# Small-head attention of a decoder: keys spread by unit of scores, values in halves behind the first scores, softmax sums inverted by batches

## The chip, the cores and the metric

The kernel runs on one core of a Trainium2 chip. The metric is the device time of one execution in microseconds. The kernel is one program for a whole decoder of four layers; the change touches three of its twelve stages.

## The reference, cut to what matters

Eight sequences of 56 tokens, width 256, pass through four layers of attention, cross-attention and feed-forward, each followed by a residual addition and a layer norm. The change touches the two attentions of layer 1 and the attention of layer 2. All of them are softmax attentions with many small heads:

```python
def _L1_attn_ref(...):                  # 32 heads of 8
    result, ch_bias, n = _chunk_decompose(hidden_states.reshape(bsz * tgt, H))
    def proj(w_orig, w_dq_t, b):
        y = result @ w_dq_t + ch_bias @ w_orig.astype(jnp.float32).T
        return y.reshape(-1, H)[:n] + b
    Q = (proj(q_weight, WQ, q_bias) * scaling).reshape(bsz, tgt, HEADS, HEAD_DIM)
    K = proj(k_weight, WK, k_bias).reshape(bsz, tgt, HEADS, HEAD_DIM)
    V = proj(v_weight, WV, v_bias).reshape(bsz, tgt, HEADS, HEAD_DIM)
    attn = jnp.einsum('bqhd,bkhd->bhqk', Q, K)
    probs = jax.nn.softmax(attn, axis=-1)
    ctx = jnp.einsum('bhqk,bkhd->bqhd', probs, V).reshape(bsz * tgt, H)
    r2, cb2, n2 = _chunk_decompose(ctx)
    out = (r2 @ WO + cb2 @ o_weight.astype(jnp.float32).T).reshape(-1, H)[:n2] + o_bias

def _L1_xattn_ref(q, latent_kv, Wq, Wkv_expand, Wout):     # 16 heads of 16
    qp = q @ Wq.T
    kv = latent_kv @ Wkv_expand.T       # keys and values come from a context of width 64
    ...                                 # causal softmax attention
    return out @ Wout.T

def _L2_attn_ref(x, q_w, kv_w, c_w):    # 16 heads of 16, 4 key/value heads
    ...                                 # rotary embedding of q and k, causal softmax attention
    return out @ c_w.T
```

`_chunk_decompose` cuts the 448 tokens into 14 chunks of 32, subtracts from each chunk and channel the middle of its range (`ch_bias`), and quantises the rest to int4 and back. A projection is then the product of the quantised residual with the quantised weight, plus the product of the 14 middles with the original weight, plus a bias.

## The kernel before, in words

**Layout.** Tokens lie in four tiles of 112 (two sequences each). `xT` holds the activations with channels on partitions, 128 x 2 x 448. PSUM has eight banks; in these three stages two pairs of banks (`bank2`) and two single banks (`bank`) turn around, and two banks hold the running output `ps_o`.

**Projections of the first stage** (`l1_attn`). `decompose` makes the residual `res` and the middles. `middles` multiplies the middles with the original weights and adds the bias: one product at a time, 14 rows, into `gb`, which is zeroed to 128 rows so that it can serve as a third term of every projection with `sel` (which chunk a token belongs to). The projection gives k, then q, each in two halves of 128 channels.

**Masked keys.** With heads of 8 or 16 channels a TensorE product over one head alone would use few rows. So `head_keys` builds `KX`: every key repeated once per head of a group and multiplied by a mask (`hm8`, `hm16`) that keeps the channels of one head. VectorE makes the first half of the sequences and POOL the second. `head_values` does the same for values: products for all eight sequences into `ps_v`, copied into a zeroed `VX` by ScalarE and VectorE.

**The loop** (`small_heads`) runs over units. A unit is a tile (two sequences) and, with heads of 8, one half of the channels: 8 units in the first stage, 4 in the two others. `scores(n)` forms the scores of a unit in PSUM, then VectorE takes maxima (`mx`) and subtracts them (`E`), ScalarE takes the exponent in place, VectorE sums (`sums`). `turned(n)` transposes the unit on TensorE and copies it to `eT`; `outputs(n)` multiplies with `VX` into `ps_o`. In program order, TensorE does scores n+1, the transposes of n, the outputs of n−1. `keep_in_program_order` fixes this order of TensorE; the other engines' orders, and where other TensorE work goes between, come from a list scheduler that estimates times. `ordered` fixes an instruction behind the one that precedes it on its engine.

**Behind the loop** all sums are inverted at once (128x128), transposed (`ps_rec`), spread into a block form `recT` by four scalings, and multiplied with a `spread` matrix into `ps_den`, the reciprocals by channel and token; VectorE multiplies them with the outputs into `oT`.

**Around it.** `finish` does the output projection (`ps_y`, tile by tile), residual addition and statistics, then `norm` (the L417 to L422 steps on few elements, the normalisation of X at L459), then `turn_x`, the transposition into `xT`. The second stage, `l1_xattn`, begins with the key projection from the context (`ps_k`), its masks and values, and the query projection from `xT`. `l2_attn` projects q and k with and without swapped pairs, multiplies with the tables (`d`, VectorE) and adds (POOL). Weights of a stage are loaded on the SP queue while the stage before runs.

Of the kernel before, what the change touches and what calls it, by code (L numbers as in the profile page):

```python
# [9 lines left out]
F32 = mybir.dt.float32  # L10
# [134 lines left out]
def _pack(i):  # L145
# [41 lines left out]
    w["l1a_s"] = _beside(_spread(8), (np.arange(T)[None, :] // 32 == np.arange(T // 32)[:, None]).astype(np.float32))  # L187
# [77 lines left out]
class Decoder:  # L265
# [1060 lines left out]
    def head_values(self, pool, terms, dk, groups=16):  # L1326


        nc = self.nc
        n, per = groups * dk // 2, 4  # L1330
        VX = pool.tile([128, NB, 128 // dk, 32], F32, bufs=1, name="VX")
        nc.gpsimd.memset(VX, 0.0)
        for g in range(NB // per):
            ps = self.bank("ps_v")
            for i in range(per):
                both = [terms(g * per + i, odd) for odd in range(2)]
                for k in range(len(both[0])):
                    for odd in range(2):
                        lhsT, rhs = both[odd][k]
                        nc.tensor.matmul(  # L1340
                            ps[odd * 64 : odd * 64 + S, i * n : (i + 1) * n], lhsT, rhs,
                            start=k == 0, stop=k == len(both[0]) - 1,
                        )
            for odd in range(2):
                rows = slice(odd * 64, odd * 64 + S)
                copy = nc.vector.tensor_copy if odd else nc.scalar.copy
                to, of = VX[rows, g * per : (g + 1) * per], ps[rows, : per * n]
                if dk == 8:
                    to = to.rearrange("p b (x y) n -> p (b x) y n", y=2)
                    of = of.rearrange("p (z y n) -> p z y n", y=2, n=8)  # L1350
                    for y in range(2):
                        at = 16 * y + 8 * odd
                        copy(to[:, :, y, at : at + 8], of[:, :, y, :])
                else:
                    same = 16 // groups
                    to = to.rearrange("p b (x y) n -> p (b x) y n", y=same)[:, :, :, 16 * odd : 16 * odd + 16]
                    of = of.rearrange("p (z n) -> p z n", n=16).unsqueeze(2).to_broadcast([S, per * groups // 2, same, 16])
                    copy(to, of)
        return VX

    def head_keys(self, pool, k, dk):

        nc, n = self.nc, 64 // dk
        KX = pool.tile([128, 2, NB, n, S], F32, bufs=1, name="KX")
        hm = self.const(f"hm{dk}").unsqueeze(1).unsqueeze(3).to_broadcast([128, NB // 2, n, S])
        for half in range(2):
            bs = slice(half * NB // 2, (half + 1) * NB // 2)
            for c in range(2):
                of = k[:, c, :].rearrange("p (b s) -> p b s", s=S)[:, bs].unsqueeze(2).to_broadcast([128, NB // 2, n, S])
                (nc.gpsimd if half else nc.vector).tensor_tensor(KX[:, c, bs], of, hm, ALU.mult)  # L1370
        return KX
# [7 lines left out]
    def small_heads(self, pool, q, KX, VX, dk, causal, scale, spread, oT):  # L1379
# [11 lines left out]
        num = pool.tile([128, 2, T], F32, bufs=1, name="num")  # L1391
# [59 lines left out]

        scores(0)
        for n in range(len(units)):
            if n + 1 < len(units):
                scores(n + 1)
            turned(n)
            if n:
                outputs(n - 1)
        outputs(len(units) - 1)
        rec = sums.rearrange("p t i -> p (t i)")  # L1460
        nc.vector.reciprocal(rec, rec)
        ps = self.bank("ps_rec")
        nc.tensor.transpose(ps[:, :128], rec, ident)
        recT = pool.tile([128, NT, 2, S], F32, bufs=1, name="recT")
        of = ps[:, :128].rearrange("p (u q) -> p u q", u=2)[:, :, :S]
        for t in range(NT):
            nc.vector.tensor_scalar_mul(recT[:, t], of, self.const("blocks")[:, t : t + 1])
        nc.scalar.copy(num, acc[:, :, :T])
        for c in range(2):
            ps = self.bank("ps_den")  # L1470
            self.mm(ps[:, :T], [(spread[:, c * 128 : (c + 1) * 128], recT.rearrange("p t u q -> p (t u q)"))])
            nc.vector.tensor_tensor(oT[:, c, :], ps[:, :T], num[:, c, :], ALU.mult)
# [54 lines left out]
    def l1_attn(self):  # L1527
# [6 lines left out]
        spread, sel = self.fields("l1a_s", D, T)  # L1534
        with tc.tile_pool(name="l1a", bufs=2) as pool:
# [20 lines left out]
            def middles(mid, first, n):  # L1556

                out = pool.tile([128, n, D], F32, bufs=1, name="gb")
                nc.gpsimd.memset(out, 0.0)
                ps = self.bank2("ps_gb")  # L1560
                for j in range(n):
                    self.mm(
                        ps[:G, j // 2, j % 2 * D : (j % 2 + 1) * D],
                        [(mid[:, c * G : (c + 1) * G], wT(first + j, c)) for c in range(2)]
                        + [(self.ones[:1, :G], bias[:, (first + j) * D : (first + j + 1) * D])],
                        fixed=True,
                    )
                for j in range(0, n, 2):
                    m = min(2, n - j)
                    nc.scalar.copy(out[:G, j : j + m, :].rearrange("p j n -> p (j n)"), ps[:G, j // 2, : m * D])  # L1570
                return out

            mid = self.decompose(pool, self.xT, res)
            gb = middles(mid, 0, 3)
            q, k = self.head_queries(pool), pool.tile([128, 2, T], F32, bufs=1, name="k")
            for m in (1, 0):
                ps = self.bank2("ps_q1")
                for o in range(2):
                    at = slice(o * 128, (o + 1) * 128)
                    self.mm(ps[:, o, :T], [(dT[:, m, c, at], res[:, c, :]) for c in range(2)] + [(gb[:, m, at], sel)])  # L1580
                    if m:
                        nc.scalar.copy(k[:, o, :], ps[:, o, :T])
                    else:
                        nc.scalar.copy(q[:, o, :, :S], ps[:, o, :T].rearrange("p (b s) -> p b s", s=S))
            KX = self.head_keys(pool, k, 8)

            def value_terms(b, odd):
                at = slice(b * S, (b + 1) * S)
                own = lambda a: a.rearrange("p (x y n) -> p x y n", y=2, n=8)[:, :, odd, :]
                return [(res[:, c, at], own(dT[:, 2, c, :])) for c in range(2)] + [(sel[:, at], own(gb[:, 2, :]))]  # L1590

            VX = self.head_values(pool, value_terms, 8, 32)
            oT = pool.tile([128, 2, T], F32, bufs=1, name="oT1")
            self.small_heads(pool, q, KX, VX, 8, False, 8.0**-0.5, spread, oT)
            res2 = pool.tile([128, 2, T], F32, bufs=1, tag="res", name="res2")
            mid = self.decompose(pool, oT, res2)
            gb2 = middles(mid, 3, 1)
            self.finish(
                early=False,
                terms_of=lambda t: [(res2[:, c, self.tok(t)], dT[:, 3, c, :]) for c in range(2)] + [(sel[:, self.tok(t)], gb2[:, 0, :])]  # L1600
            )


    def l1_xattn(self):
        nc, tc, xT = self.nc, self.tc, self.xT
        wq, wo = self.fields("l1x_1", 512, 512)
        wk, wv, cT = self.fields("l1x_2", D, D, T)
        wq, wo = (a.rearrange("p (c n) -> p c n", c=2) for a in (wq, wo))
        (spread,) = self.fields("l1x_t", D)
        with tc.tile_pool(name="l1x", bufs=2) as pool:  # L1610
            q = self.head_queries(pool)
            k = pool.tile([128, 2, T], F32, bufs=1, name="k")
            qps, kps = self.bank2("ps_q"), self.bank2("ps_k")
            for o in range(2):
                self.mm(kps[:, o, :T], [(wk[:DC, o * 128 : (o + 1) * 128], cT[:DC, :])])
            nc.scalar.copy(k, kps[:, :, :T])
            KX = self.head_keys(pool, k, 16)

            def value_terms(b, odd):
                own = wv[:DC, :].rearrange("p (x y n) -> p x y n", y=2, n=16)[:, :, odd, :]  # L1620
                return [(cT[:DC, b * S : (b + 1) * S], own)]

            VX = self.head_values(pool, value_terms, 16)
            for o in range(2):
                at = slice(o * 128, (o + 1) * 128)
                self.mm(qps[:, o, :T], [(wq[:, c, at], xT[:, c, :]) for c in range(2)])
                nc.scalar.copy(q[:, o, :, :S], qps[:, o, :T].rearrange("p (b s) -> p b s", s=S))
            oT = pool.tile([128, 2, T], F32, bufs=1, name="oT")
            self.small_heads(pool, q, KX, VX, 16, True, 0.25, spread, oT)
            self.finish(lambda t: [(oT[:, c, self.tok(t)], wo[:, c, :]) for c in range(2)], early=False)  # L1630


    def l2_attn(self):
# [6 lines left out]
        with tc.tile_pool(name="l2a", bufs=2) as pool:  # L1640
# [12 lines left out]
            KX = self.head_keys(pool, k, 16)  # L1653
            terms = lambda b, odd: [(xT[:, c, b * S : (b + 1) * S], wv[:, c, :]) for c in range(2)]
            VX = self.head_values(pool, terms, 16, 8)
            oT = pool.tile([128, 2, T], F32, bufs=1, name="oT2")
            self.small_heads(pool, q, KX, VX, 16, True, 0.25, spread, oT)
            self.finish(lambda t: [(oT[:, c, self.tok(t)], wo[:, c, :]) for c in range(2)], early=False, turn=False)
# [240 lines left out]
```

## Time and profile before

| | |
|---|---|
| time, three runs | 1656.13, 1664.53, 1664.38 us (median 1664.38) |
| profiled execution | 1665.35 us, span 1663.1 us |
| mean granted TensorE clock | 0.926 |
| PE busy | 90% |
| VectorE, ScalarE, POOL busy | 66%, 38%, 19% |
| first touched stage, loop | 535 to 566 us |
| second touched stage, loop | 607 to 625 us |
| third touched stage, loop | 754 to 772 us |

The shares are means over the whole span. The three loops together last some 68 us, and in them no engine is full for long: they pass each unit from one to the next. The granted clock of TensorE is 1.00 or 0.50 in a single stretch of the trace, and 0.926 is its mean.

### The profile page before, as it was taken

To read this page: it belongs to the slowest core of one execution; us is meant where nothing else is said; L and a number is where in the kernel's file an instruction comes from. 1 tells how busy PE (TensorE), PEld (TensorE's weight loads), DVE (VectorE), ACT (ScalarE), POOL (GpSimd) and SP (SyncE) were. 2 spreads that over 40 slices of the span, in tenths; PEclk is the share of its full clock that TensorE was granted. 3 is DMA by queue.
4 is the path that set the end of the run, shared out by engine and by line. 5 is a ranking of instruction groups with operands and counts; after the bars stand their busy time and mean duration, and the time that the engine had idled before them with its cause. 6 is when DMAs were issued, how large, how long until landed. Compare 5 with 4: busy or idle time off the path is not lost.

```text
span 1663.1 us, 37875 instructions
## 1 busy us (share of the span) xinstructions
PE 1499.5 (90%) x16428; PEld 894.4 (54%) x16428; DVE 1095.2 (66%) x1793; ACT 625.2 (38%) x915; POOL 323.9 (19%) x302
## 2 busy tenths in 40 slices
PE   7989989999788678998989999899987978999898
PEld 4666435556644344565435555655555834555656
DVE  0575579999475855326569999635474239999633
ACT  2431245655312422103245556332343144566320
POOL 4711511212123010011521122101131000221200
PEclk9999979999897878999988999999997987999989
DMA  9523422323020001222332322121220361323100
GB/s 359 188 79 108 123 56 84 96 83 88 18 87 28 26 27 35 78 70 74 114 86 62 110 78 81 41 64 55 83 64 27 119 172 38 104 72 88 41 1 11
DMA packets 52088, 133.76 MB, mean 80 GB/s; under 512 B 20673, under 2 KB 21137, under 8 KB 51922
## 3 DMA queue, kind: packets, MB, share of 16 engines
q1 hardware_dynamic: 19906, 65.36, 12.0%
q10 hardware_dynamic: 28368, 50.25, 10.8%
q0 software_dynamic: 3648, 15.73, 2.9%
q8 instruction: 129, 2.11, 0.5%
q14 instruction: 37, 0.30, 0.1%
HBM read 119.06 MB, written 6.75 MB: 76 GB/s over the span
## 4 chain that ended last, share of the span: by engine, by line
PE 49%; DVE 9%; issue 8%; ACT 2%; DMA 1%; POOL 1%; ACTq 1%; DVEq 0%; POOLq 0%
PE ps_x L376 17%; PE ps_glu L368 8%; PE ps_y L368 7%; PE ps_qk L1675 2%; DVE sc L376 2%; PE ps_v L1675 2%; PE ps_qh L368 2%; PE ps_big L368 1%; PE ps_y L1675 1%; PE ps_q L368 1%; PE ps_qk L376 1%; PE ps_m L376 1%; PE ps_s L1397 1%; DVE E L1418 1%; DVE mx L1415 1%
## 5 line engine op out<-in xcount | busy, mean ns | idle before, releaser
L376 PE MATMUL ps_x<-kvT,qa 64*128 64x375 f32 x1344 | 310.4, 567 | 29.1 <-DVE sc L376 23.1
L376 ACT ACTIVATE sc<-sc,tops 128x1500 f32<-128x1500 f32 x168 | 259.2, 1544 | 151.7 <-DVE sc L376 118.3
L376 DVE STREAM_TRANSPOSE eT<-sc 128x1536 f32<-128x1536 f32 x168 | 297.1, 1768 | 11.7 <-PE ps_x L376 9.5
L376 PE MATMUL ps_x<-eT,kv 32*64 32x224 f32 x9024 | 257.7, 357 | 3.7 <-issue 3.2
L376 PEld LDWEIGHTS ps_x<-eT,kv 32*64 32x64 f32 x9024 | 197.6, 133 | 70.1 <-issue 59.8
L376 PEld LDWEIGHTS ps_x<-kvT,qa 64*128 64x128 f32 x1344 | 114.3, 201 | 187.2 <-DVE sc L376 160.4
L376 DVE TENSOR_SCALAR_CACHE_REDUCE sc<-ps_x 128x750 f32<-128x750 f32 x168 | 157.3, 936 | 38.4 <-PE ps_x L376 38.2
L376 DVE TENSOR_SCALAR_CACHE_REDUCE sc<-ps_x,tops 128x750 f32<-128x750 f32 x168 | 161.1, 959 | 1.3 <-PE ps_x L376 1.1
L376 POOL TENSOR_TENSOR eT<-eyes,sums 128x224 f32<-128x224 f32 x24 | 13.3, 555 | 453.6 <-DVE sums L376 453.6
L827 POOL TENSOR_TENSOR rope<-rope,turn 96x448 f32<-96x448 f32 x64 | 71.0, 1130 | 65.0 <-DVE turn L825 65.0
L824 DVE TENSOR_TENSOR rope<-ps_big,consts 96x896 f32<-96x896 f32 x32 | 34.8, 1086 | 58.4 <-PE ps_big L368 58.4
L1190 ACT ACTIVATE act<-ps_glu 128x448 f32<-128x448 f32 (+1 forms) x52 | 28.3, 544 | 111.7 <-PE ps_glu L368 108.4
L1194 DVE TENSOR_TENSOR act<-ps_glu,act 128x448 f32<-128x448 f32 x43 | 26.8, 624 | 65.2 <-ACT act L1190 65.1
L418 ACT ACTIVATE rstd<-rstd 112x3 f32<-112x3 f32 (+2 forms) x21 | 4.3, 204 | 166.2 <-DVE rstd L417 166.1
L624 DVE RECIPROCAL rec<-rec 128x896 f32<-128x896 f32 x8 | 46.0, 5753 | 27.0 <-ACT rec L623 27.0
L376 PE MATMUL ps_x<-wm,qa 128*112 128x128 f32 (+1 forms) x336 | 53.5, 318 | 9.7 <-DVE qa L376 9.7
L450 DVE TENSOR_TENSOR X<-X,ps_y 112x256 f32<-112x256 f32 x32 | 13.5, 421 | 70.6 <-PE ps_y L368 70.6
L376 PEld LDWEIGHTS ps_x<-wm,qa 128*112 128x112 f32 x336 | 45.2, 191 | 21.7 <-issue 11.2
L1758 POOL TENSOR_TENSOR qk<-qk,sw 128x896 f32<-128x896 f32 x16 | 33.3, 2083 | 101.3 <-DVE sw L1757 78.8
L376 POOL TENSOR_TENSOR qa<-num,rec 64x448 f32<-64x448 f32 x42 | 47.9, 1140 | 2.9
L754 ACT COPY qa<-ps_qk 64x448 f32<-64x448 f32 x48 | 25.3, 527 | 60.0 <-PE ps_qk L376 46.1
L376 POOL DMA_DIRECT2D kvT<-kvT x24 | 13.7, 573 | 122.7 <-DVE X L450 49.2
(410 smaller groups left out, 2424.2 us busy)
## 6 DMA issues: line engine op xcount, KB each, us to landing
kv<-kv ACTq DMA_DIRECT2D x288, 128.0 KB, 2.7
kvT<-kvT POOLq DMA_DIRECT2D x24, 384.0 KB, 3.5
qa<-qa ACTq DMA_DIRECT2D x24, 224.0 KB, 3.6
raw<-in_ctx ACTq DMA_DIRECT2D x6, 512.0 KB, 4.3
kv<-raw POOLq DMA_DIRECT2D x6, 512.0 KB, 4.2
kvT<-by POOLq DMA_DIRECT2D x6, 512.0 KB, 4.3
l0a_q<-in_l0a_q SPq DMA_DIRECT2D x4, 512.0 KB, 10.6
l0a_c<-in_l0a_c SPq DMA_DIRECT2D x4, 512.0 KB, 8.8
```

The lines of the kernel that those rows point to most:

```text
L368: ins = self.nc.tensor.matmul(out, lhsT, rhs, start=n == 0, stop=n == len(terms) - 1)
L376: call(*args, **kw)
L624: nc.vector.reciprocal(rec, rec)
L754: nc.scalar.copy(flat[rows, :, odd, h // 2 * S : (h // 2 + 1) * S], ps[rows, :T].rearrange("p (b s) -> p b s", b=NB))
L824: nc.vector.tensor_tensor(rope.rearrange("p a (b s) -> p a b s", b=NB), view, cos, ALU.mult)
L827: nc.gpsimd.tensor_tensor(rope[:, half, :], rope[:, half, :], turn[:, 1 - half, :], ALU.add)
L1190: nc.scalar.activation(act, ps[:m, 0, :T], AF.Silu)
L1194: nc.vector.tensor_tensor(act, ps[:m, 1, :T], act, ALU.mult)
L1397: tc.keep_in_program_order(nc.tensor.matmul(*args, **kw))
L1415: nc.vector.tensor_reduce(mx, view, AX.X, ALU.max)
L1675: tc.keep_in_program_order(nc.tensor.matmul(*args, **kw))
L1758: nc.gpsimd.tensor_tensor(qk, qk, sw, ALU.add)
```

## The change

It does the following in the three stages:

- **Middles**: the products for k, q and v lie in three groups of 32 columns of TensorE (rows 0, 32, 64 of the result), in three banks, their terms interleaved. `gb` is no longer zeroed; each projection's third term has 14 rows. `sel` is repeated every 32 rows for this.
- **Order in the first stage**: half of k, half of q, half of k, the first scores, half of q, the second scores, then the values of the first four sequences behind `scores(1)` and of the last four behind `scores(2)`.
- **Keys by unit**: VectorE makes `KX` of units 0 and 1 (both channel halves of the first two sequences) straight from PSUM; POOL makes units 2, 4 and 6; VectorE makes units 3, 5 and 7, each ordered into the loop. In the two stages with heads of 16, `KX` is made in eight parts: all on VectorE in the second stage, half on VectorE and half on POOL in the third.
- **Values**: all copies into `VX` on ScalarE.
- **Sums**: inverted tile by tile in the loop, transposed in four pieces into 32 rows, copied once, and multiplied with 32 rows of `spread`.
- **Context's keys and values** (`l1x_context`): made at the end of the first stage's attention, ahead of its second `decompose`; the pool of the second stage is opened before that of the first.

```diff
 # head_keys
-        for half in range(2):
-            bs = slice(half * NB // 2, (half + 1) * NB // 2)
-            for c in range(2):
-                of = k[:, c, :].rearrange("p (b s) -> p b s", s=S)[:, bs].unsqueeze(2).to_broadcast([128, NB // 2, n, S])
-                (nc.gpsimd if half else nc.vector).tensor_tensor(KX[:, c, bs], of, hm, ALU.mult)
-        return KX
+        def made(unit, of_, engine):
+            t, cs = (unit // 2, (unit % 2,)) if dk == 8 else (unit, range(2))
+            for c in cs:
+                of = of_(c).rearrange("p (b s) -> p b s", s=S)[:, 2 * t : 2 * t + 2]
+                engine.tensor_tensor(KX[:, c, 2 * t : 2 * t + 2], of.unsqueeze(2).to_broadcast([128, 2, n, S]), hm, ALU.mult)
+        return KX, made
 # head_values: made(g) is called for half g
-                copy = nc.vector.tensor_copy if odd else nc.scalar.copy
+                ...  nc.scalar.copy(to, of)
 # small_heads
+        keys(0)
         scores(0)
         for n in range(len(units)):
             if n + 1 < len(units):
+                if not n:
+                    keys(1)
                 scores(n + 1)
+            if n < 2:
+                VX = values(n)
             turned(n)
             if n:
                 outputs(n - 1)
+            if n + 2 < len(units):
+                keys(n + 2)
+            if n % per == per - 1:
+                nc.vector.reciprocal(sums[:, n // per], sums[:, n // per])
         outputs(len(units) - 1)
-        rec = sums.rearrange("p t i -> p (t i)")
-        nc.vector.reciprocal(rec, rec)
+        nc.scalar.copy(num, acc[:, :, :T])
         ps = self.bank("ps_rec")
-        nc.tensor.transpose(ps[:, :128], rec, ident)
...
+            tc.keep_in_program_order(nc.tensor.transpose(ps[:32, t * 128 : (t + 1) * 128], sums[:, t], ident))
+        recT = pool.tile([32, NT * 2, S], F32, bufs=1, name="recT")
+        nc.vector.tensor_copy(recT, ps[:32].rearrange("p (u q) -> p u q", q=64)[:, :, :S])
 # l1_attn
+            def middles(mid, ms):
+                out = pool.tile([128, D], F32, bufs=1, name="gb")
+                ps = self.bank2("ps_gb")
+                banks = [ps[:, 0], ps[:, 1], self.bank("ps_gb1") if len(ms) > 2 else None]
+                for k in range(3):
+                    for j, m in enumerate(ms):
+                        ...
+                        self.ordered(nc.tensor.matmul, banks[j][32 * j : 32 * j + G, :D], lhsT, rhs, start=k == 0, stop=k == 2)
+                for j in range(len(ms)):
+                    nc.scalar.copy(out[32 * j : 32 * j + G], banks[j][32 * j : 32 * j + G, :D])
+                return lambda j: (out[32 * j : 32 * j + G], sel[32 * j : 32 * j + G])
...
+            def keyed(o):
+                ps = projected(0, 1, o)
+                made(o, lambda c: ps[:, :T], nc.vector)
+                nc.scalar.copy(k[:, o, :], ps[:, :T])
+            def keys(n):
+                if n == 0:
+                    keyed(0)
+                    projected(1, 0, 0)
+                    keyed(1)
+                    for m in (2, 4, 6):
+                        made(m, lambda c: k[:, c, :], nc.gpsimd)
+                elif n == 1:
+                    projected(1, 0, 1)
+                elif n % 2:
+                    self.ordered(made, n, lambda c: k[:, c, :], nc.vector)
...
             self.small_heads(pool, q, KX, keys, values, 8, False, 8.0**-0.5, spread, oT)
+            self.l1x_context()
             res2 = pool.tile([128, 2, T], F32, bufs=1, tag="res", name="res2")
 # l1_xattn
+            for n in range(NT):
+                made(n, lambda c: k[:, c, :], nc.vector)
 # l2_attn
+            for n in range(NT):
+                made(n, lambda c: k[:, c, :], nc.gpsimd if n > 1 else nc.vector)
```

## The prediction

> **What bounds the kernel now.** I read the shares first, then the chain of waits through the changed stages, then VectorE's timeline and TensorE's clock by window. The page's first part:
>
> ```profile
> PE 1499.5 (90%) x16428; PEld 894.4 (54%) x16428; DVE 1095.2 (66%) x1793; ACT 625.2 (38%) x915; POOL 323.9 (19%) x302
> ```
>
> PE is busy for 90% of the span, but that is an average: the cross-attentions and the feed-forwards fill it. The three stages that the change touches lie at about 501–597, 597–639 and 736–779 us, some 180 us of 1663. The chain of waits there (start, duration, what):
>
> ```profile
> 508.94 8.32 PE ps_gb L368 x18
> 517.26 9.69 PE ps_q L368 x18
> ...
> 530.20 4.94 PE ps_v L1340 x86
> 535.14 1.66 PE ps_s L1397 x16
> ...
> 545.05 0.96 PE ps_s L1397 x8
> 546.03 1.09 DVE mx L1415
> 547.12 0.99 DVE sums L1420
> 548.11 1.01 DVE E L1418
> 549.14 0.96 ACT E L1419
> 550.14 1.09 PE ps_eT L1430 x8
> 551.24 0.57 PE ps_o L1397 x31
> 551.80 0.95 PE ps_s L1397 x8
> ...
> 592.96 0.70 DVE VX L1358
> 593.88 0.70 DVE VX L1358
> ...
> 597.82 3.35 PE ps_k L368 x4
> ```
>
> Up to 536 us PE alone sets the time: bias middles, key and query projections, values, scores. From there the softmax loop is a ring through all three engines: scores, maxima, the previous unit's sums, subtraction, exponent, transposes, outputs, scores. One turn is 551.80 − 545.05 = 6.75 us and serves two units: 3.37 each, of which VectorE has 3.09 (1.09 + 0.99 + 1.01). VectorE is nearly full in this loop and PE is not. The last three lines show two VX copies that VectorE makes inside the norm, and a key projection at the entry of the second stage: both leave this path.
>
> VectorE's timeline at the key masks:
>
> ```profile
> 522.64 2.03 DVE L1370 TENSOR_TENSOR KX<-k,consts 128x1792 f32<-128x1792 f32 x1 [7.31 <-ACT k L1582]
> 526.05 3.55 DVE L1370 TENSOR_TENSOR KX<-k,consts 128x1792 f32<-128x1792 f32 x1 [1.38 <-ACT k L1582]
> ```
>
> The same operation took 2.03 and 3.55 us; POOL made its own half of KX from 522.69 to 532.66. TensorE's clock by window (length, then busy time of PE, PEld, DVE, ACT, POOL, then the granted clock):
>
> ```profile
> 515.89:519.31 3.42, 3.42 (x6) 1.30 (x6) 0.00 (x0) 0.84 (x2) 0.00 (x0) 0.50 0.13 53
> 519.31:522.72 3.41, 3.41 (x6) 1.41 (x5) 0.08 (x1) 0.53 (x1) 0.03 (x1) 0.50 0.00 0
> 522.72:526.13 3.41, 3.41 (x11) 1.75 (x10) 2.03 (x2) 0.53 (x1) 3.41 (x1) 1.00 0.00 0
> ...
> 560.27:563.68 3.41, 1.68 (x41) 1.37 (x41) 2.40 (x4) 1.92 (x3) 0.00 (x0) 1.00 0.00 0
> 563.68:567.09 3.41, 2.62 (x73) 2.09 (x73) 2.75 (x6) 1.88 (x3) 0.00 (x0) 1.00 0.02 5
> ...
> 590.99:594.40 3.41, 1.48 (x28) 1.23 (x24) 2.94 (x8) 1.16 (x3) 1.62 (x5) 1.00 0.50 161
> 594.40:597.81 3.41, 1.76 (x8) 1.38 (x8) 1.55 (x5) 0.91 (x1) 0.00 (x0) 0.50 0.00 0
> ```
>
> The clock changes at multiples of 3.41 us. Two full windows at 0.50 stand before the rise; a window with PE 1.68 busy (49%) kept full clock for the next, one with 1.48 (43%) lost it.
>
> **The change part by part**, against the profiled execution (1665.35 us: span 1663.1 and 2.25 around it; the median shown is 0.97 lower).
>
> *Middles and start.* The POOL memset of gb (0.74) and that of VX (3.51) leave the norm ahead, where one X operation lasted 2.26 instead of 0.42; part of this remains since the VX memset is only moved. I take −0.7. The three middles in column groups no longer end behind the residual: it is ready at 515.33, ps_gb ended at 517.26, so the projections start up to 1.9 us sooner.
>
> *Order up front, tiled attention.* New PE order: k half 0, q half 0, k half 1, scores 0, q half 1, scores 1, values half 0, transposes 0, scores 2, values half 1. VectorE makes KX 0 and 1 straight from PSUM (128x896, nearest row mx from PSUM, 1.09), while ACT's key copies (0.53) wait for it; POOL makes 2, 4, 6 (2.5 each, half of its 5.03), ahead of need. I laid the operations out by hand with the durations shown. With the clock rising at 522.7, as it does now, scores 3 start at 542.1; they started at 545.05: −2.9.
>
> *Rule against row.* Two full windows precede the rise at 522.72. The Trainium skill, "TensorE: Matmul & The Clock Gate", "What's actually happening", says that one busy window of about 3.4 us is enough, free-running. The first of the two held 1.4 us of 14-column middles, so it may not have counted; with middles gone from it the rule gives a rise at 519.3 and scores 3 at 540.4 (−4.6). But a third of each projection's terms now has 14 rows instead of 128 zero-padded ones. I stay with the row; the rule's 1.7 goes into the range.
>
> *The loop.* VectorE's queue in the built program reads: sums 2, KX 3, mx 3, E 3, mx 4, sums 3, E 4, reciprocal, sums 4, KX 5, mx 5 and so on. KX 3, 5 and 7 (1.09 each, half of 2.03 with its start) stand behind the sums of the unit before and ahead of their own scores. So scores 5 wait for KX 5, KX 5 for sums 4, these for exponent 4. One turn becomes a single file: KX 1.12, scores 0.98, mx 1.12, E and mx 2.1, the interposed sums 1.0, E 1.1, exponent 1.0, sums 1.0, with their gaps 9.7 us for two units against 6.75. Queued behind the waiting KX are its own mx and all later ones; PE waits for scores, and its transposes follow. Two such turns (KX 3 to 5, 5 to 7): +5.9. VectorE has only 7.9 us of work per turn, so 1.8 of the 9.7 is waiting. At the end: of four reciprocals of 128x32 (estimate 0.35, from 0.33 for 128x28) only the last is on the path, in place of one of 0.95, and one copy of 32x448 (0.63) replaces four scalings (1.07); with the last turn's overlap −1.4. From scores 3 to oT: 29.4 against 24.9, +4.5.
>
> *Rule against row again.* PE then works 5.2 us of a turn of 9.7 (twice 0.96, 1.09 and 0.57), 54% on average, and by the layout rests for 3.9 in one piece ahead of scores 5 and of scores 7. The same page, "HAM oscillation — how this bites in real kernels", warns of idle gaps above about 3.4 us: by it both gaps cost the clock, a cold window each of transposes, outputs and scores, +3 to +4. By the rows only the share of a window counts, with its limit between 43% and 49%; a gap that falls across two windows may pass, and part of a cold window is waiting anyway. I go by the rows and take +2 (ends 0 and +4). Stage so far: −0.7 − 2.9 + 4.5 + 2.0 = **+2.9**.
>
> *Context's keys and values.* k projection, values and four VX copies (0.58 each, ACT) move between oT and the second decompose, where PE waits 4.9 us for VectorE: nothing, while the top transpose (due 574.18) stands behind under 4 us of them; without that cover up to +1. ACT is free there. But in the norm chain VectorE now has eight KX of 128x448 (estimate 0.55–0.63, from 1.09 for twice as much) between X of the last tile, its statistics and the reciprocal: +4.4. Gone from there: two VX copies (−1.4), and of the 0.92 of L417, waiting beside POOL's memset, 0.75. Net **+2.1**; ends 0 (if statistics wait for ps_y anyway) and +3.
>
> *Entry of the second stage.* The 3.35 us of ps_k before ps_q are gone: −3.35. But these were the busy time that let the second query half run at 1.77 instead of 3.35, and KX is no longer the wait: I give back 2.4, for a later rise through scores 0 and transposes 0. **−0.95**; ends −3.4 and +1. Its loop: four reciprocals +0.5, end −0.45, **+0.2**.
>
> *Rope attention.* Rows of now: values 752.51 to 754.44, scores 0, E 1 at 759.16, scores 2 at 760.1. Values now come behind scores 1; the four VX copies (0.58) stand on ACT between exponent 0, exponent 1 and the transposes' copies, VectorE's half is lost, and transposes 1 wait for a bank until those copies are through: scores 2 at 762.7, +2.1 after a reciprocal's share. KX in eight parts: two multiplications of the rope for q stand on VectorE behind KX parts that wait for POOL's second k (749.05), +0.4. POOL's two KX of 1.3 precede its q additions, due by 753, as 2.59 did. **+2.5**; ends −1 and +3.5.
>
> Sum: 2.9 + 2.1 − 0.95 + 0.2 + 2.5 = +6.75, so 1672.1 against the profiled run, 1671.1 against the median. What a measurement of this kernel can tell from no change is about 0.5%, 8.3 us.
>
> **The rivals.**
>
> *Faster: VectorE's new work falls into waits that it has anyway.* Then KX 5 and 7 cost only VectorE's fill, a turn is 7.9 (+2.4 − 1.4 in place of +4.5) and PE's rests are too short for a cold window; half of the norm's KX hides (+1.0), and the rope multiplications wait for nothing (−1). With the clock up at 519.3 (−4.6) and kept at the entry (−3.35): −0.7 − 4.6 + 1.0 + 1.0 − 3.35 − 1 = −7.65, or 1656–1657, on the edge of 0.5%. For it: the lead of 3 to 5 us up front, and POOL ahead of need. Against: the queue order, in which KX 5 follows sums 4. It decides for this side if scores 5 start within 8 us of scores 3.
>
> *Slower: the clock stays half.* If 14-row terms don't count as work, projections, values and the output projection (a third of the terms each) stay cold. Each lost window up front costs 1.7 by my layout; three of them +5, ps_y cold to its end +3: 1672 + 8 = 1680. For it: ps_gb, 100% busy from 509 to 516 at 0.50. Against: two thirds of the terms are as before.
>
> *Nothing:* gains and losses within 2 us of zero, if loop and lead cancel and norm and entry too: 1663–1666.
>
> **How the numbers follow.** Serial keys as summed 0.48; faster rival 0.17; clock rival 0.22; nothing 0.13. The likeliest is 1671, own range 1666 to 1676, on both sides of the bound at 1672.7. Faster by over 0.5% (below 1656): most of the faster rival and surprises, 0.16. Slower (over 1672.7): clock rival and under half of the main case, 0.43. Within: 0.41. The range holds 8 in 10 from 1656 to 1684.
>
> **What would show it.** In the changed profile: scores 3 at 540–542 less the start's shift; 9–10 us between KX 3, KX 5 and KX 7, idle before KX put to exponent or sums; granted clock 0.5 in a window inside the loop; eight KX between ps_y's end and xT; no ps_k behind xT; in the rope stage scores 2 later by 2–3 us. Turns of 8 us or a rope loop no longer than 19.6 would prove me wrong.

## The result, and the profile after

The changed kernel takes 1681.62 us (median of 4 runs, 1679.55 to 1688.02) against 1663.64 for the kernel before: a ratio of 1.0129, with a 95% interval from 1.0093 to 1.0165. It is 1.3% slower, some 18 us, where 6.75 were forecast.

The page's first part hardly differs; the loss cannot be read from shares:

```profile
PE 1504.8 (90%) x16437; PEld 892.8 (53%) x16437; DVE 1088.5 (65%) x1796; ACT 629.5 (38%) x924; POOL 313.1 (19%) x301
```

So I cut both profiles into stretches, each from the start of one instruction to the start of another. "Before again" is a second profile of the kernel before (experiment e12), to show how far two profiles of one kernel differ.

| stretch, us | before | before again | changed | forecast of the difference |
|---|---|---|---|---|
| first stage: last step of the residual to oT | 54.4 | 53.0 | 62.7 | +3.6 (without the earlier start) |
| oT to the second residual's last step | 11.9 | 11.9 | 14.4 | 0 |
| that step to the end of ps_y | 9.5 | 9.6 | 13.6 | 0 |
| end of ps_y to the copy of xT | 6.9 | 6.9 | 8.0 | +2.1 |
| second stage: xT to the first scores | 10.3 | 10.3 | 9.0 | −0.95 |
| first scores to the next xT | 31.2 | 31.3 | 30.9 | +0.2 |
| rope stage: first projection to first scores | 17.9 | 17.9 | 19.7 | +2.5 for the whole stage |
| its first scores to oT | 19.8 | 19.8 | 25.3 | |
| its oT to the next stage's first product | 4.6 | 4.6 | 6.3 | |
| sum | 166.5 | 165.2 | 189.8 | |

(The first scores are the first products with KX; decompose is the step from oT to the residual.) The touched stages lost 23 to 25 us. The rest moved too: −7.9 ahead of the first stage, +1.6 between the second and the rope stage and −2.6 behind the last against the first profile (−3.9 and +0.5 at the two ends against the second). Of the −7.9 only the last norm belongs to the change: its four X operations took 2.62 us instead of 3.30, the forecast −0.7. Hence the stretches, and not the totals, are compared below.

Stretches of the same code differ between profiles as well: the changed kernel's first stage to oT is 62.7 to 62.9 in five of them and 65.9 in e7, its second stage (xT to xT) 39.3 to 43.1 and its rope stage 48.3 or 51.2. A difference within such a spread is not a finding.

Chain of waits of the changed kernel, first stage (start, duration, what):

```profile
507.58 9.90 PE ps_q L369 x18
...
522.64 3.78 PE ps_v L1346 x48
526.50 0.63 ACT VX L1359 x2
527.13 0.85 ACT E L1430
528.00 0.65 ACT VX L1359 x2
528.70 1.12 PE ps_eT L1441 x4
...
545.72 1.09 DVE sums L1431
546.81 1.01 DVE KX L1380
547.86 0.98 PE ps_s L1408 x8
...
557.05 1.09 DVE sums L1431
558.14 1.01 DVE KX L1380
559.19 1.68 PE ps_s L1408 x8
...
584.52 12.48 PE ps_y L369 x24
```

Three things are to be seen: half of the values takes 3.78 us and is followed by copies and an exponent in one ScalarE queue before the second half of the transposes can start; KX stands between sums and scores, and the scores of units 5 and 7 are 11.3 us apart (547.86 to 559.19) where a turn was 6.75; and ps_y, 8.35 before, takes 12.48. The clock in the loop and in ps_y (length, busy time of PE, PEld, DVE, ACT, POOL, granted clock):

```profile
545.23:548.65 3.42, 0.79 (x8) 0.21 (x8) 2.08 (x2) 0.46 (x1) 0.00 (x0) 1.00 0.00 0
548.65:552.06 3.41, 3.41 (x48) 2.39 (x48) 2.18 (x2) 1.96 (x3) 0.00 (x0) 0.57 0.00 0
...
555.47:558.89 3.42, 0.00 (x0) 0.00 (x0) 2.66 (x4) 0.95 (x1) 0.00 (x0) 1.00 0.00 0
558.89:562.30 3.41, 3.11 (x15) 1.72 (x16) 1.59 (x3) 0.29 (x1) 0.00 (x0) 0.57 0.00 0
...
586.19:589.61 3.42, 3.42 (x8) 1.53 (x7) 1.03 (x3) 0.00 (x0) 0.00 (x0) 0.50 0.02 5
589.61:593.02 3.41, 3.41 (x8) 1.82 (x8) 1.03 (x3) 0.00 (x0) 0.00 (x0) 0.50 0.00 0
593.02:596.43 3.41, 3.41 (x8) 1.63 (x7) 1.03 (x3) 0.00 (x0) 0.00 (x0) 0.50 0.00 0
```

Both rests in the loop (3.83 and 4.72 us, ahead of scores 5 and 7) cost the following window its clock. And ps_y holds PE busy without a gap for three whole windows, at half clock to the last.

### The profile page after: what moved, and what is told of

The parts are those of the page before. It is cut to its first block, busy times and chain, and to the rows that moved or that the text cites. A ratio compares the mean times of both kernels' runs of the same rounds, so it can differ in the third digit from the quotient of the medians.

```text
span 1677.5 us, 37899 instructions
## 1 busy us (share of the span) xinstructions
PE 1504.8 (90%) x16437; PEld 892.8 (53%) x16437; DVE 1088.5 (65%) x1796; ACT 629.5 (38%) x924; POOL 313.1 (19%) x301
## 3 DMA queue, kind: packets, MB, share of 16 engines
q1 hardware_dynamic: 19906, 65.36, 11.9%
HBM read 119.06 MB, written 6.75 MB: 75 GB/s over the span
## 4 chain that ended last, share of the span: by engine, by line
PE 49%; DVE 9%; issue 8%; ACT 3%; DMA 1%; ACTq 1%; POOL 1%; DVEq 0%; POOLq 0%
PE ps_x L377 16%; PE ps_glu L369 8%; PE ps_y L369 7%; PE ps_qk L1728 2%; DVE sc L377 2%; PE ps_v L1728 2%; PE ps_qh L369 2%; PE ps_big L369 1%; PE ps_q L369 1%; PE ps_y L1728 1%; PE ps_s L1408 1%; PE ps_qk L377 1%; PE ps_v L1346 1%; PE ps_m L377 1%; PE ps_qk L369 1%
## 5 line engine op out<-in xcount | busy, mean ns | idle before, releaser
L377 PEld LDWEIGHTS ps_x<-wm,qa 128*112 128x112 f32 x336 | 43.5, 186 | 20.7 <-issue 11.1
L755 ACT COPY qa<-ps_qk 64x448 f32<-64x448 f32 x48 | 25.3, 527 | 59.8 <-PE ps_qk L377 43.3
L815 ACT COPY qh<-ps_qh 128x448 f32<-128x448 f32 x32 | 17.0, 532 | 55.0 <-PE ps_qh L369 55.0
```

Source lines behind the costliest of these rows:

```text
L377: call(*args, **kw)
L755: nc.scalar.copy(flat[rows, :, odd, h // 2 * S : (h // 2 + 1) * S], ps[rows, :T].rearrange("p (b s) -> p b s", b=NB))
L815: nc.scalar.copy(qh, ps[:, :T])
```

## The experiments

The edits e1 to e4 each undo one part; the totals (ratios 1.0116 to 1.0184, intervals from ±0.0045 to ±0.0072) are too coarse to tell them apart from the changed kernel (1.0129), so each is judged by the stretches of one profile. e7, e8, e10, e11 and e12 ran once, for the profile alone; their times are not compared.

**e1: POOL makes all keys of the loop.**

```diff
-                    for m in (2, 4, 6):
+                    for m in range(2, 8):
                         made(m, lambda c: k[:, c, :], nc.gpsimd)
...
-                elif n % 2:
-                    self.ordered(made, n, lambda c: k[:, c, :], nc.vector)
```

> The changed kernel with one edit: KX of units 3, 5 and 7 of the first stage is made by POOL behind 2, 4, 6, and nothing of KX is in VectorE's queue within the loop. Theory A (KX behind the sums serialises the loop): scores 3 to 5 and 5 to 7, now 9.8 and 11.3 us, fall to 6.7 to 7.0 each, the cold windows inside the loop go, the stage is 7 to 9 us shorter and the time about 1674. Rival B (the loop is long because PE is at half clock and the transposes wait for PSUM banks, wherever the keys are made): turns stay above 9 and the time moves by less than 2 us.

Chain of waits of e1:

```profile
547.44 0.96 PE ps_s L1408 x8
...
554.20 0.96 PE ps_s L1408 x8
```

Scores 5 and 7 are 6.76 us apart: the turn of before. The first stage falls from 62.7 to 54.2. No window of the loop from scores 3 on is cold, and the loop takes 23.9 us from there to the end of oT, where it was 32.2. Theory A holds: the keys in VectorE's queue cost 8.5 us, cold windows included. Time 1679.35 against 1658.28 of the kernel before on that chip, ratio 1.0116 [1.0059, 1.0172]: neither the forecast 1674 (about 1.006) nor no gain at all can be told from it.

**e2: gb padded to 128 rows.**

```diff
-                out = pool.tile([128, D], F32, bufs=1, name="gb")
+                out = pool.tile([128, len(ms), D], F32, bufs=1, name="gb")
+                nc.gpsimd.memset(out, 0.0)
...
-                return lambda j: (out[32 * j : 32 * j + G], sel[32 * j : 32 * j + G])
+                return lambda j: (out[:, j, :], sel)
```

> The changed kernel with gb zero-padded to 128 rows again (one 128-row tile for each of the middles, zeroed by POOL), so that the third term of projections, values and ps_y has 128 rows; all else as changed. Theory A (terms of 14 rows do not count as work for the clock): the output projection ps_y falls from 12.5 us, all at clock 0.50, to 8 to 9.5 with the clock at 1.00 in its second half, and a half of the values from 3.8 to about 2.7; 5 to 8 us less in all. Rival B (the clock is low because PE idled and ran the 64-row context products before): ps_y stays above 11.5 at 0.50 and the time moves by less than 2 us.

TensorE's timeline at the first and the third tile of ps_y, changed kernel and then e2 (start, duration, line, operation, shapes, records):

```profile
584.52 2.05 PE L369 MATMUL ps_y<-dT,res 128*112 128x256 f32 x4 [3.68 <-DVE res L1502]
586.49 1.19 PE L369 MATMUL ps_y<-gb,l1a_s 14*112 14x256 f32 x2
...
590.71 2.05 PE L369 MATMUL ps_y<-dT,res 128*112 128x256 f32 x4
592.69 1.19 PE L369 MATMUL ps_y<-gb,l1a_s 14*112 14x256 f32 x2
```

```profile
586.44 2.05 PE L369 MATMUL ps_y<-dT,res 128*112 128x256 f32 x4 [3.67 <-DVE res L1502]
588.28 1.06 PE L369 MATMUL ps_y<-gb,l1a_s 128*112 128x256 f32 x2
...
591.69 1.06 PE L369 MATMUL ps_y<-dT,res 128*112 128x256 f32 x4
592.59 0.59 PE L369 MATMUL ps_y<-gb,l1a_s 128*112 128x256 f32 x2
```

With 128 rows the third tile runs at twice the speed; with 14 it does not. The stretch to the end of ps_y is 9.2 against 13.6, the first stage 59.3 against 62.7. Both ran the same cold context products ahead of it, so rival B falls. Half of the values takes 2.79 instead of 3.78. The time (ratio 1.0163 [1.0118, 1.0208]) does not show the 7.8 us (3.4 to oT and 4.4 to ps_y's end); only the stretches do.

**e3: the second stage's KX on POOL** (`nc.gpsimd` for `nc.vector` in `l1_xattn`).

> The changed kernel with the eight KX operations of the second stage on POOL instead of VectorE; POOL starts them when k is copied, beside the second decompose. Theory A (eight KX on VectorE stretch the norm): from the last X addition to the copy of xT 4 to 5 us less[...], time 2 to 4 us less. Rival B (the norm waits for something else[...]): decompose longer by 3 or more and the time within 1.5 us.

POOL's timeline in e3:

```profile
602.10 7.26 POOL L1380 TENSOR_TENSOR KX<-k,consts 128x448 f32<-128x448 f32 x8 [77.72 <-PE ps_y L369]
```

A miss for both. POOL didn't start when k was copied: its queue stood for 77.7 us and went on when the last product of ps_y had ended. KX lies in a pool that is opened after the first stage's pool is closed; a wait on ps_y fits a tile that takes over the place of gb, dT or the residual, which ps_y reads to the end. So "ahead" stops at keys and values; with the tile placed there, KX itself can't be made before ps_y ends, on any engine. From ps_y's end to xT it took 9.0 instead of 8.0, and the time (ratio 1.0184 [1.0112, 1.0256]) is no better. (Putting KX in the earlier pool wasn't tried.)

**e4, e7, e11: the rope stage, keys and values as before, together and apart.**

```diff
-            for n in range(NT):
-                made(n, lambda c: k[:, c, :], nc.gpsimd if n > 1 else nc.vector)
+            KX, keys = self.head_keys_halves(pool, k, 16), lambda n: None   # keys: e4, e7
...
+            for g in range(2):
+                values(g)                                                  # values: e4, e11
```

> The changed kernel with the rope stage's keys and values as before the change: KX in two halves of the sequences (VectorE, POOL), values ahead of the first scores, their copies shared by ScalarE and VectorE; its sums stay inverted tile by tile. Theory A (order of queues: rope multiplications behind KX that waits for POOL, exponent's table load behind the subtraction, transposes' bank behind VX copies): stage from xT to the next stage's first product falls from 51.3 to 42 to 43.5 us, time 7 to 9 less. Rival B (a cold clock at entry makes most of it): it falls to 46 to 49 only.

> The changed kernel with the rope stage's KX alone as before (two halves of the sequences, VectorE and POOL); its values stay behind the first scores. Theory A (two costs in that stage, apart): its entry is shorter by 1 to 3.5 us (TensorE no longer waits for the rope multiplication behind KX), its loop stays near 25 us. Rival B (the values' order makes it all): entry within 0.5 of the changed kernel's.

> The changed kernel with the rope stage's values alone as before: ahead of the first scores, copies shared by ScalarE and VectorE; its KX stays in eight parts. Theory A (values behind scores cost the table load and the transposes' bank): from its first scores to oT about 21 against 25.3, its exponent table is loaded before the first subtraction ends; entry as in the changed kernel plus 1.9 for the values. Rival B (KX in parts makes the loop late): the loop stays above 24.

| rope stage, us | to first scores | to oT | to next product | sum |
|---|---|---|---|---|
| before | 17.9 | 19.8 | 4.6 | 42.3 |
| changed; same code in e1, e2, e3 | 19.7; 17.0 | 25.3; 25.3 | 6.3; 6.0 | 51.2; 48.3 |
| e4, both as before | 16.2 | 21.1 | 6.3 | 43.5 |
| e7, keys | 14.2 | 27.4 | 6.1 | 47.8 |
| e11, values | 19.0 | 21.8 | 6.9 | 47.7 |

Together they give back 4.8 to 7.7 us and theory A's figure for e4 is met (43.5), with a tail that stays long; each alone gives 0.5 to 3.5, which the spread of 2.9 between profiles of the same code nearly covers. That spread stands in the entry (19.7 and 17.0). The total of e4 (ratio 1.0118 [1.0073, 1.0163]) doesn't show the gain. With the keys alone the entry is shorter and the loop, against expectation, longer by 2.1: scores come sooner, and the values that stand behind them hold them up. The two places in the changed kernel, VectorE's timeline and ScalarE's:

```profile
758.24 0.62 DVE L1380 TENSOR_TENSOR KX<-k,consts 128x448 f32<-128x448 f32 x1 [1.91 <-POOL k L1704]
758.78 0.62 DVE L1702 TENSOR_TENSOR d<-ps_qk,consts 128x448 f32<-128x448 f32 x1
```

```profile
769.34 1.28 ACT L1430 ACT_TABLE_LOAD   x1 [24.32 <-DVE E L1429]
770.63 1.79 ACT L1430 ACTIVATE E<-E 128x896 f32<-128x896 f32 x2
```

A rope multiplication `d`, whose bank TensorE needs, stood behind a KX that waited 1.91 us for POOL, and TensorE then waited 2.03 and ran its next window (760.7 to 764.1) at half clock. The load of the exponent's table (1.28) began only when the subtraction had ended; in e4 it came ahead of it:

```profile
762.44 0.58 ACT L1364 COPY VX<-ps_v 56x512 f32<-56x512 f32 x1 [0.24 <-PE ps_v L1346]
763.03 1.28 ACT L1442 ACT_TABLE_LOAD   x1
766.11 0.95 ACT L1442 ACTIVATE E<-E 128x896 f32<-128x896 f32 x1 [1.79 <-DVE E L1441]
```

In e7, with values behind, it is exposed again (18.86 us idle, then the load behind the subtraction); in e11, with values ahead, it stands behind a copy and is not: the values' order decides. Why the load itself waits for the subtraction where no copy stands ahead of it was not taken apart; the traces show only that it does.

**e5: the kernel before with thin terms.** The third term reads 14 rows instead of 128, the rest of which are zeros:

```diff
-+ [(gb[:, m, at], sel)])
++ [(gb[:G, m, at], sel[:G])])
...
-+ [(sel[:, self.tok(t)], gb2[:, 0, :])]
++ [(sel[:G, self.tok(t)], gb2[:G, 0, :])]
```

> The kernel before with one edit: the third term of projections, values and output projection reads 14 rows of gb and sel instead of 128 (the same sum, since the rest is zeros). Theory A (a term of 14 rows weighs little for the clock, and it costs its own time): ps_y goes from 8.4 us to 11.5 to 12.5 at 0.50 throughout, the values from 5.7 to 7 or more, the clock in the projections rises no earlier than now; 4 to 8 us slower in the stage. Rival B (ps_y is cold in the changed kernel for what stands before it): ps_y within 8.0 to 9.5 and the time within 2 us.

TensorE's clock in e5 while ps_y runs:

```profile
585.40:588.80 3.40, 3.40 (x8) 1.51 (x6) 1.03 (x3) 0.00 (x0) 0.00 (x0) 0.50 0.01 2
588.80:592.20 3.40, 3.40 (x8) 1.67 (x8) 1.03 (x3) 0.00 (x0) 0.00 (x0) 0.50 0.00 0
```

The strongest run: in the kernel before, with nothing else changed, the stretch to ps_y's end goes from 9.5 to 13.6 and the first stage from 53.0–54.4 to 58.3 (25.5 + 32.8), a little more than the 4 to 8 expected. The values take 6.92 us instead of 4.94 (86 products). All touched stretches together are 176.3, +9.8 to +11.1, and the time agrees: 1672.94 against 1663.02, ratio 1.0075 [1.0052, 1.0098]. Reading zeros was faster than leaving them out.

**e8: the second stage as before** (context's keys and values in their own stage, KX in halves).

> The changed kernel with the second stage alone as before (context's keys and values in their own stage, KX in halves on VectorE and POOL). Theory A (made ahead, the context's products stand before the transpose that the second decompose waits for, and KX cannot start before ps_y ends): decompose from oT to residual 14.4 falls to 12, from ps_y's end to xT 8.0 to about 7, and 1 to 1.5 us come back at the entry; 2 to 3 less in all. Rival B (decompose is long for another reason): it stays above 13.5.

From oT to the residual 11.9 instead of 14.4, from ps_y to xT 7.8 instead of 8.0, from xT to the scores 10.3 instead of 9.0: 1.4 us back, less than expected, and none in the sum: the second stage's loop came out 1.6 longer, and all touched stretches make 189.9 against 189.8. (The key masks left the norm, but the context's values, at half clock, took their place there.) Theory A is right in kind for decompose. But e7 and e10 have the context products ahead and a decompose of 11.9 too. TensorE's timeline of the changed kernel, then of e10:

```profile
569.56 3.35 PE L369 MATMUL ps_k<-l1x 64*128 64x448 f32 x4
572.85 3.66 PE L1346 MATMUL ps_v<-l1x 64*56 64x128 f32 x32
576.44 0.38 PE L1525 MATMUL ps_top<-consts,t 128*14 128x128 f32 x1
```

```profile
572.50 1.77 PE L369 MATMUL ps_k<-l1x 64*128 64x448 f32 x4
574.20 1.96 PE L1346 MATMUL ps_v<-l1x 64*56 64x128 f32 x32
577.56 0.27 PE L1526 MATMUL ps_top<-consts,t 128*14 128x128 f32 x1 [1.40 <-DVE t L1524]
```

At full clock the products take 3.7 us, and ps_top waits for VectorE; at half clock 7.0, and VectorE waits for ps_top. The cover was there, for a warm clock only. The trace also tells where the clock went: in the changed kernel the window ahead of these products (566.17 to 569.59) was 80% busy, 1.7 us of it with the spread products (`ps_den`) on 32 rows, and the next one was cold; in e10, with spread products on 128 rows, a window 64% busy (569.14 to 572.55) kept it.

**e10: the changed kernel with the sums as before; e6 and e9: what paid, together.** e6 keeps the changed middles, the order in front of the first loop and the sums by tiles; it has e1's keys, e2's padding, e4's rope stage and e8's second stage. e9 is e6 with one reciprocal of 128x128, one transpose, four scalings and spread products of 128 rows.

> The parts that paid, together: the changed kernel's middles, its order in front of the first loop, and its sums by tiles stay; gb is zero-padded to 128 rows, POOL makes KX of units 2 to 7, and the second and third stage have keys and values as before. Theory A (the costs found are the four: keys in the loop, thin terms, context ahead, rope order): residual to oT in the first stage 49 to 51 us against 54.4 before, ps_y about 9, the other stages as before or 0.5 shorter; 3 to 6 us faster than before. Rival B (the front, with exponents and value copies in one ScalarE queue, eats the lead): 53 to 55 us there and no difference beyond 2 us.

> The changed kernel with the sums inverted and spread as before, all else as changed. Theory A as for e9: oT to the next product in the rope stage 4.6 against 6.25, its loop shorter by up to 1; the first stage's tail longer by 1. Rival B: those two figures within 0.5 of the changed kernel's.

> The combined version (e6) with the sums inverted and spread as before the change: one reciprocal of 128x128 behind the loop, one transpose, four scalings, spread products with 128 rows. Theory A (four reciprocals in the loops and spread products of 32 rows lose the clock ahead of the output projections): the second and third stage go back to before's figures, oT to xT 10.5 against 11.7, rope loop 19.8 against 21.7, oT to the next product 4.6 against 6.8; the first stage gives back about 1; 3 to 5 us faster than e6 and 4 to 6 faster than before. Rival B (those cold stretches are the phase of the clock's windows): stages differ by less than 1 in sum and the time within 2 us of e6's.

| us | first stage to oT | second stage: xT to xT | rope stage | touched, sum |
|---|---|---|---|---|
| before; again | 54.4; 53.0 | 41.5; 41.6 | 42.3; 42.3 | 166.5; 165.2 |
| e6 | 49.8 | 44.6 | 44.8 | 166.1 |
| e9 | 50.3 | 40.1 | 42.3 | 159.7 |

(The sum has the stretches from oT to xT in the first stage too: 28.2 before, 27.0 in both.) The first stage gains what the lead promised, 2.7 to 4.6 us. In e6 the other two stages ate it up; with the old sums they are back. For the second stage that is weaker than it looks: the code of before has 41.5, 41.6, 42.4 (e5) and 40.1 (e9) there, with the new sums 42.8 (e8) and 44.6 (e6), and one code alone has spread by 3.8. For the rope stage it is clear. Rope stage, TensorE's timeline, e6 and then e9:

```profile
767.59 3.35 PE L369 MATMUL ps_den<-recT,l2a 32*128 32x448 f32 x4 [0.70 <-DVE recT L1500]
770.87 5.54 PE L369 MATMUL ps_y<-l2a,oT 128*112 128x256 f32 x16
```

```profile
763.64 1.74 PE L369 MATMUL ps_den<-recT,l2a 128*128 128x448 f32 x4 [1.24 <-DVE recT L1500]
765.42 3.96 PE L369 MATMUL ps_y<-l2a,oT 128*112 128x256 f32 x16
```

Every profile with the sums by tiles has 5.9 to 6.9 us from the rope stage's oT to the next product (nine of them), every one with the old sums 4.56 or 4.57 (before, again, e5, e9, e10). That is no accident of phase. The clock by window, changed kernel and then before, from the spread products on:

```profile
788.04:791.45 3.41, 2.67 (x9) 0.97 (x7) 1.86 (x3) 1.88 (x2) 0.00 (x0) 1.00 0.00 0
791.45:794.86 3.41, 3.41 (x8) 2.58 (x9) 1.36 (x5) 0.00 (x0) 0.00 (x0) 0.50 0.00 0
```

```profile
771.89:775.30 3.41, 2.17 (x16) 0.87 (x8) 1.67 (x5) 2.19 (x2) 0.00 (x0) 1.00 0.00 0
775.30:778.71 3.41, 3.37 (x15) 2.48 (x15) 2.54 (x8) 0.00 (x0) 0.00 (x0) 1.00 0.00 0
```

The busier window lost the clock: in seven of the nine a window 78 to 90% busy, with 1.7 to 1.8 us of spread products on 32 rows, was followed by a cold one, and with the old sums a window 62 to 64% busy, on 128 rows, was not. In the other two (e6, e11) a window 35 or 44% busy had lost it already, and the spread products ran cold. So the traces point to the 32 rows and not to later transposes or idle time; no run separates the two, and in the changed kernel's second stage a window with 1.35 us of such products kept the clock.

Of e10's expectations the rope tail came true (4.57); its rope loop, 25.5 against 25.3, did not get shorter.

In time, e6 stands at 0.9989 [0.9973, 1.0005] and e9 at 0.9984 [0.9966, 1.0002] of the kernel before. The 5.5 to 6.8 us that e9 gains in the touched stretches is 0.3 to 0.4%, and the interval reaches from 0.34% faster to no gain: it isn't shown to be faster. Nor is e9 shown to be faster than e6: the two ratios differ by 0.0005.

**e12: before again.**

> The kernel before once more, for a second profile: how far stages that no kernel changed, and the touched ones, differ between two profiles of one kernel. If the clock's phase alone moves them, the start of the first touched stage (503.7 in the first profile) and the rest behind (884) move by several us, the touched stages by less than 3.

The first touched stage begins at 499.7 instead of 503.7, the rest behind is 880.7 instead of 883.8, the touched stretches differ by 1.3, all of it in the first stage's projections.

## Why the prediction was wrong, point by point

The ring of waits in the loop was right. What failed is the price of narrow products: the main sum gave products of 14 rows (and the new sums' 32) no cost, neither in time nor for the clock ("two thirds of the terms are as before", "only the share of a window counts"), and left that to a rival. The touched stretches lost 23.3 us where 7.45 were forecast (the 6.75 without the 0.7 gained ahead of them). Of the 15.9 that were missing, the front has 3.8, the output projection 4.1 and the context products 2.5, all three under narrow products; e2 gives back 7.8 by padding alone. The rope stage, mis-sized, has 6.4. By the steps:

- **Order up front: −2.9 forecast, +0.9 measured.** From the residual's end (507.44) to scores 3 (538.07) it took 30.6 us, before (515.33 to 545.05) 29.7. The layout used the durations of before, and 86 value products took 4.94 there, so some 2.8 for half of the values; with thin terms they took 3.78 and 4.05. ScalarE's queue, with value copies and exponents ahead of the transposes' copies, held the second half of the transposes twice. In e2, where nothing but the padding differs, the same stretch is 26.3: the −2.9 was right for a kernel with terms of 128 rows.
- **Rule against row, the rise of the clock.** I stayed with the row (two windows). The Trainium skill's rule ("TensorE: Matmul & The Clock Gate", "What's actually happening": one busy window is enough) came true in the changed kernel's own profile, where the clock rose at 511.56, one full window after 508.15. That was luck of the phase. e4 has the same code up to here, and its rise came a full window later, at 516.19. TensorE's timeline, changed kernel and then e4:

```profile
507.58 3.32 PE L369 MATMUL ps_q<-res,dT 128*128 128x448 f32 x4 [3.74 <-DVE res L1502]
510.83 1.36 PE L369 MATMUL ps_q<-l1a_s,gb 14*128 14x448 f32 x2
```

```profile
508.33 3.32 PE L369 MATMUL ps_q<-res,dT 128*128 128x448 f32 x4 [3.74 <-DVE res L1514]
511.59 1.86 PE L369 MATMUL ps_q<-l1a_s,gb 14*128 14x448 f32 x2
```

  The window to 511.56 held 0.73 us of 14-row products, 21% of it; e4's window to 512.78, just as busy, held 1.19 us, 35%, and no rise followed. e3, e10 and e11 went as e4; e1, e7 and e8 as the changed kernel. So one busy window isn't always enough here; the doubt about the thin terms was right, and was left out of the sum.
- **The loop: +4.5 and +2 for the clock.** From scores 3 to the end of oT 32.2 us against 24.9: +7.3 for a forecast of +6.5. KX stood where the queue order put it, turns were 9.8 and 11.3, and both long rests (3.83 and 4.72) cost a window, as the same page warns ("HAM oscillation — how this bites in real kernels"); by it I should have taken +3 to +4. The limit on busy time that I read from the rows, between 43% and 49%, doesn't hold here: the changed kernel lost the clock after windows 52% busy (525.21 to 528.63, rest of 1.72) and 80% busy (566.17 to 569.59, no rest above 0.71). e1 shows the whole cost.
- **The output projection: 0 in the main sum.** It was put into a rival as "ps_y cold to its end +3". Measured +4.1, and e2 and e5 show the cause. Here the step fails most plainly: ps_gb, 14 columns wide, busy and cold from 509 to 516, had shown already that full windows of narrow products don't raise the clock, and I took the two thirds of full terms for enough.
- **Context ahead: 0, "without that cover up to +1"; measured +2.5.** The cover of 4.9 us was measured against products at full clock; they ran at half.
- **Norm: +2.1 forecast, +1.2 measured. Entry: −0.95 forecast, −1.3 measured.** As reasoned. (The norm's own terms make 2.25 and those of the second loop 0.05 instead of 0.2; the two slips cancel.)
- **Rope stage: +2.5 forecast, +8.9 measured** (+6.0 in e1 to e3 with the same code). The waiting rope multiplication was seen and priced at +0.4; it made TensorE wait 2.03 and restart cold. The table load was not seen: it cost nothing before, because it stood behind a copy and ahead of the wait. The tail, +1.7, was not foreseen: the shorter sums chain had been booked as a gain. Scores 2 came 4.1 later where 2 to 3 were forecast.

The faster rival's condition (scores 5 within 8 us of scores 3) was not met: 9.8. The clock rival named the cause that the main sum left out, but that its 1680 lies near the result is luck in part: the projections did warm up in this profile, and a good part of the excess stands in the rope stage, for which it had nothing.

## What to carry to other kernels

A product with few rows is not cheaper here: it takes no less time and keeps the clock down, so a term padded with zeros can be the faster one. When work moves in front of something, recompute its cover at half clock, and look what the moved work did for others where it stood: a copy that hid a table load, a product that kept the clock up. And before an operation is put "in the loop", write down its engine's whole queue for one turn: what stands behind a sum waits for the exponent.

## What the runs showed of the hardware that was not expected

- Busy time alone does not raise TensorE's clock. ps_y with a third of its records on 14 rows stayed at 0.50 through 12.5 us without a gap (changed kernel, e1, e3, e4, e5 and others: 13.6 us each time for the stretch); with zeros in the other 114 rows it rose in about 5 us (e2). The projections have the same third, and the window decided: of the cold windows that TensorE filled with projections or ps_y and 14-row terms, those with up to 22% of their time in such terms (each product counted to the start of the next) were followed by full clock (eight profiles), those with 33% or more were not (ps_y 33 to 42%; projections 35 to 39% in e3, e4, e10, e11 and 52% in e5). Between the two these runs have nothing, and other mixes need not follow it: full windows of scores (64 x 64), transposes (128 x 128) and outputs (128 x 32) in the loop were followed by full clock as well (changed kernel, 549.11).
- Nor does busy time alone keep it. A window 80% busy with 1.7 us of 32-row products lost it, one 64% busy with 128 rows kept it (changed kernel 566.17, e10 569.14).
- A thin term isn't faster even at full clock: two records of 14 rows and 448 columns took 1.01 us where 128 rows took 0.92, half of the values with 14-row terms 3.78 against 2.79 in e9.
- A table load can be hidden or exposed without any change to the activation that needs it.
